# The expert layer of a convolution-attention block: seven block products with sums on VectorE and GpSimd in place of eight, and the next image's tokens turned between the two layers

## Chip, cores and metric

One core of a Trainium2 chip runs the whole program. The metric is the device time in microseconds, the median of several runs. Engine names are short below: PE is TensorE, DVE is VectorE, ACT is ScalarE, Pool is GpSimd, SP is SyncE, which issues nearly all of the DMAs here.

## What is computed

Eight images of 32x32 positions (1024 tokens) with 256 channels pass a convolution with attention, an attention layer, and then a layer of experts with a layer norm. The change is in the experts only. For these the reference has

```python
h = gelu(einsum('nd,edf->enf', xf, W1) + b1[:, None, :])          # D = 256, F = 512, E = 8
y = einsum('enf,efd->end', h, W2) + b2[:, None, :]
out = einsum('ne,end->nd', w_dense, y)                             # two experts of eight have a weight
out = layer_norm(out + x, gamma, beta)
```

The routing is worked out from the mean of an image, so all 1024 tokens of an image use the same two experts. The kernel computes just these two. All numbers are float32.

## The kernel before, in words

The first 1,923 us of the kernel, the convolution and both attentions, are scheduled by hand and are not touched. They leave the tokens of each image in DRAM (`Td`) and the mean and scale of each token's norm in `mv2`.

The stage of the experts (from line 1243) is written as a plain loop over the images b (from line 1417), in which the framework orders the instructions: each engine gets its instructions one after another from a list, by the place that they have in the program. One that is not ready, because its data or a buffer of its pool is missing, is passed by, and a later one goes ahead. The order is fixed when the kernel is built; on the chip every engine works through its own queue in order. A pool's `bufs` says how many buffers a tile name has. A buffer is given to the next tile when the last reader of the tile before it is done.

For image b the loop does this:

- `load_image(b + 1)` (line 1273) has SP load the next image's tokens `T2` (1 MB), and `load_experts(b + 1)` (line 1376) the two experts' `w1` and `w2` (512 KB each); Pool scales `w2` by the routing weight (line 1390). All have two buffers.
- `turn` (line 1278) makes the normed tokens `n2` on DVE (line 1282, eight instructions) and turns them for the matmuls: 16 transposes on PE into four tiles of pool `ps_t` (two buffers), copied out by DVE (line 1293) and ACT (line 1295) into `n2T`, 128 channels x 2 halves of channels (`kc`) x 1024 tokens. For image 0 it is called ahead of the loop, for the others at the head of their own iteration (line 1422).
- `mix` (line 1424) is a small matmul with the experts' second bias. ACT copies it to `mixed`; Pool adds it to `n2` (line 1427) and adds `beta` to `T2` (line 1428).
- Then, for each half q of the tokens (512 of them), the first layer: for each expert k and each of four blocks f of 128 hidden units, two matmuls of 128x128 by 128x512 into `phd` (line 1435, pool `ps_h`, three buffers) and one Gelu with bias on ACT into `hT` (line 1442). After it the second layer of the same half: four groups of eight matmuls into `py` (line 1452, pool `ps_y`, three buffers), whose results DVE adds to `n2` (line 1459, called r below), with the statistics, a square root on ACT (line 1464), and two DVE instructions per group (lines 1468 and 1469, the latter writing `yo`). SP stores `yo` (line 1472).

One float32 matmul appears as two PE records in the profile.

Of the kernel before, what the change touches and what calls it, by code (L numbers as in the profile page):

```python
# [10 lines left out]
FP = mybir.dt.float32  # L11
FR = mybir.dt.float32r
I32 = mybir.dt.int32
AF = mybir.ActivationFunctionType
ALU = mybir.AluOpType
AX = mybir.AxisListType
PSUM = bass.MemoryType.PSUM

P = 128
B, HH, WW, C = 8, 32, 32, 256  # L20
S = HH * WW
NT = S // P
KC = C // P
# [6 lines left out]
NF = F // P  # L30
TOPK = 2
# [7 lines left out]
def kernel(  # L39
# [26 lines left out]
    nc = tc.nc  # L66
# [45 lines left out]
    with ExitStack() as ph:  # L112
        wp = ph.enter_context(tc.tile_pool(name="wp", bufs=1))
        work = ph.enter_context(tc.tile_pool(name="work", bufs=1))
# [39 lines left out]
        def st_tile(name):  # L154
            return ps_st.tile([P, 512], FP, tag="st", name=name)
# [22 lines left out]
        for i, (n, table) in enumerate((("h", key_rel_h), ("w", key_rel_w))):  # L178
# [8 lines left out]
            out=rawc.rearrange("p (m o) -> p m o", o=CO), in_=conv_w.rearrange("a b (k p) o -> p (a b k) o", p=P)  # L187
# [164 lines left out]
        class Fill:  # L352
# [47 lines left out]
            def add(self, work, cost):  # L400
                self.dense.append(work)
                self.owed += cost
# [651 lines left out]
        class Attention:  # L1054
# [27 lines left out]
            def turn(self, last=False):  # L1082
                blk, i, pr = self.scored.pop(0)
                for c in range(2):
                    tp = st_tile("tp").rearrange("p (j t) -> p j t", j=4)
                    for j in range(4):
                        jc = c * 4 + j
                        te.transpose(tp[:, j, :], pr[:, jc * P : (jc + 1) * P], ident)
                    dst = blk.pt[:, c * 4 : c * 4 + 4, i * P : (i + 1) * P]
                    if c == 0 and not last:  # L1090
                        nc.vector.tensor_copy(dst, tp)
                    else:
                        nc.scalar.copy(dst, tp)
                if self.turned:
                    self.turned.pop(0).finish()
                if i == NIB - 1:
                    self.turned.append(blk)
# [146 lines left out]
    fw = ctx.enter_context(tc.tile_pool(name="fw", bufs=2))  # L1244
    work = ctx.enter_context(tc.tile_pool(name="fwork", bufs=2))
    ps_t = ctx.enter_context(tc.tile_pool(name="ps_t", bufs=2, space=PSUM))
    ps_h = ctx.enter_context(tc.tile_pool(name="ps_h", bufs=3, space=PSUM))
    ps_y = ctx.enter_context(tc.tile_pool(name="ps_y", bufs=3, space=PSUM))

    wr = small.tile([P, KC, E], FP, tag="wr", name="wr")  # L1250
    nc.sync.dma_start(out=wr, in_=w_r.rearrange("(k p) e -> p k e", p=P))
# [17 lines left out]
    def sm(shape, name):  # L1269
        return small.tile(shape, FP, tag=name, name=name)  # L1270


    def load_image(b):
        t = work.tile([P, NT, C], FP, tag="T2", name="T2")
        nc.sync.dma_start(out=t, in_=Td[b])
        return t

    def turn(b, Tb):
        n2 = work.tile([P, NT, C], FP, tag="n2", name="n2")
        n2T = work.tile([P, KC, S], FP, tag="n2T", name="n2T")  # L1280
        for t in range(NT):
            nc.vector.tensor_scalar(
                n2[:, t, :], Tb[:, t, :], mv2[:, b, t, 0:1], mv2[:, b, t, 1:2], ALU.subtract, ALU.mult
            )
        for kc in range(KC):
            for q in range(2):
                tp = ps_t.tile([P, 4, P], FP, tag="t", name="tp2")
                for j in range(4):
                    nc.tensor.transpose(tp[:, j, :], n2[:, q * 4 + j, kc * P : (kc + 1) * P], ident)
                dst = n2T[:, kc, q * 512 : (q + 1) * 512]  # L1290
                src = tp.rearrange("p j t -> p (j t)")
                if q == 0:
                    nc.vector.tensor_copy(dst, src)
                else:
                    nc.scalar.copy(dst, src)
        return n2, n2T

    tn = load_image(0)
    plog = ps_t.tile([P, 512], FP, tag="t", name="plog")
# [76 lines left out]
    def load_experts(b):  # L1376
        ws = []
        for k in range(TOPK):
            n = k * B + b
            e = nc.sync.value_load(idx_i[0:1, n : n + 1], min_val=0, max_val=E - 1)  # L1380
            w1t = fw.tile([P, KC, F], FP, tag=f"w1_{k}", name=f"w1_{k}")
            nc.sync.dma_start(
                out=w1t, in_=w1[bass.ds(e, 1), :, :].rearrange("o (k p) f -> p (o k) f", p=P)
            )
            w2t = fw.tile([P, NF, C], FP, tag=f"w2_{k}", name=f"w2_{k}")
            nc.sync.dma_start(
                out=w2t, in_=w2[bass.ds(e, 1), :, :].rearrange("o (f p) d -> p (o f) d", p=P)
            )

            nc.gpsimd.tensor_scalar(w2t, w2t, wbc[:, n : n + 1], None, ALU.mult)  # L1390
            ws.append((w1t, w2t))
        return ws

    nxt = load_experts(0)
    turned = turn(0, tn)
    gelu = sm([B, TOPK], "gelu")
    nc.scalar.activation(gelu, wt, AF.Gelu)
# [16 lines left out]
    b1c = sm([P, NF, TOPK * B], "b1c")  # L1414
    nc.vector.tensor_copy(b1c, pb)

    for b in range(B):
        ws, Tb = nxt, tn
        if b + 1 < B:
            tn = load_image(b + 1)  # L1420
            nxt = load_experts(b + 1)
        n2, n2T = turned if b == 0 else turn(b, Tb)
        mix = ps_t.tile([P, 512], FP, tag="t", name="mix")
        nc.tensor.matmul(mix[:, 0:C], lhsT=dbc[:, b, :], rhs=b2sb, start=True, stop=True)
        mixed = work.tile([P, 1, C], FP, tag="mixed", name="mixed")
        nc.scalar.copy(mixed[:, 0, :], mix[:, 0:C])
        nc.gpsimd.tensor_tensor(n2, n2, mixed.to_broadcast([P, NT, C]), ALU.add)
        nc.gpsimd.tensor_tensor(Tb, Tb, bet.to_broadcast([P, NT, C]), ALU.add)
        for q in range(2):
            hT = work.tile([P, TOPK * NF, 512], FP, tag="hT", name="hT")  # L1430
            for k in range(TOPK):
                for f in range(NF):
                    phd = ps_h.tile([P, 512], FP, tag="h", name="phd")
                    for kc in range(KC):
                        nc.tensor.matmul(  # L1435
                            phd,
                            lhsT=ws[k][0][:, kc, f * P : (f + 1) * P],
                            rhs=n2T[:, kc, q * 512 : (q + 1) * 512],
                            start=kc == 0,
                            stop=kc == KC - 1,  # L1440
                        )
                    nc.scalar.activation(  # L1442
                        hT[:, k * NF + f, :], phd, AF.Gelu, bias=b1c[:, f, k * B + b : k * B + b + 1]
                    )
            r = work.tile([P, 4, C], FP, tag="r", name="r")
            st = work.tile([P, 4, 6], FP, tag="fst", name="fst")
            mv = work.tile([P, 4, 2], FP, tag="fmv", name="fmv")
            for j in range(4):
                py = ps_y.tile([P, C], FP, tag="y", name="py")
                for k in range(TOPK):  # L1450
                    for f in range(NF):
                        nc.tensor.matmul(  # L1452
                            py,
                            lhsT=hT[:, k * NF + f, j * P : (j + 1) * P],
                            rhs=ws[k][1][:, f, :],
                            start=k + f == 0,
                            stop=k == TOPK - 1 and f == NF - 1,
                        )
                nc.vector.tensor_tensor(r[:, j, :], py, n2[:, q * 4 + j, :], ALU.add)  # L1459
                nc.vector.bn_stats(st[:, j, :], r[:, j, :])  # L1460
            for i in range(4):
                nc.vector.bn_aggr(mv[:, i, :], st[:, i : i + 1, :])
            nc.vector.tensor_scalar(mv[:, :, 1], mv[:, :, 1], 1e-5, None, ALU.add)
            nc.scalar.activation(mv[:, :, 1], mv[:, :, 1], AF.Sqrt)
            nc.vector.reciprocal(mv[:, :, 1], mv[:, :, 1])
            y = work.tile([P, 4, C], FP, tag="yo", name="yo")
            for j in range(4):
                nc.vector.scalar_tensor_tensor(r[:, j, :], r[:, j, :], mv[:, j, 0:1], gam, ALU.subtract, ALU.mult)
                nc.vector.scalar_tensor_tensor(
                    y[:, j, :], r[:, j, :], mv[:, j, 1:2], Tb[:, q * 4 + j, :], ALU.mult, ALU.add  # L1470
                )
            nc.sync.dma_start(
                out=ot[b, q * 512 : (q + 1) * 512, :].rearrange("(p k) c -> p k c", k=4), in_=y
            )
# [50 lines left out]
```

## Time and profile before

| | us |
|---|---|
| median of three runs (2415.1, 2431.19, 2431.35) | 2431.19 |
| the profiled execution: its time | 2426.65 |
| its span, first to last instruction | 2424.9 |
| PE busy in the span | 2203.9 |
| DVE busy | 1384.1 |
| ACT busy | 1041.5 |
| Pool busy | 516.6 |
| experts' stage, first matmul of `phd` to the end | 1950.5 to 2424.9 |

The profile has one line per group of instructions: line of the source, engine, operation, output and input by name, shapes and count, then the busy time in us with the mean ns of one, and the idle time of the engine ahead of them with what ended most of it. The windows view gives for a stretch of the span the busy time of PE, of PE's weight loads (PEld), DVE, ACT and Pool, each with its number of instructions, then the granted clock of PE as a share of full speed, and the DMA. The chain view follows the work that ended last back through what released it. The timeline lists start, duration, engine, line and operation.

### The profile page before, as it was taken

How to read it: one execution, taken by the hardware profiler on the slowest of the kernel's cores; microseconds unless marked ns; L12 is line 12 of the kernel's file. 1: busy time of each engine (PE TensorE's matmuls, PEld its weight loads, DVE VectorE, ACT ScalarE, POOL GpSimd, SP SyncE). 2: the span in 40 equal slices, each digit the busy share in tenths (PEclk: the TensorE clock that was granted, in tenths of full speed). 3: DMA queues.
4: the chain of work that ended last, by engine and by line, in shares of the span. 5: the costliest groups of instructions: out<-in, count | busy, mean ns of one | idle time of the engine just before them, and what ended most of it. 6: DMA issues, size and time to landing. Idle time of an engine off the chain costs nothing.

```text
span 2424.9 us, 28815 instructions
## 1 busy us (share of the span) xinstructions
PE 2203.9 (91%) x10515; PEld 1419.0 (59%) x10515; DVE 1384.1 (57%) x3147; ACT 1041.5 (43%) x1990; POOL 516.6 (21%) x446
## 2 busy tenths in 40 slices
PE   5589999899999999999899999999998789999998
PEld 4455556556555665566556556665664456666665
DVE  4667746575685666575657575657571633333333
ACT  2145544444454445444544454445454322222332
POOL 2213211320223022202120311131111042222220
PEclk7699999999999989998999899989998889999999
DMA  4634312701461245124312521361110121222210
GB/s 122 125 88 122 80 40 71 186 11 45 101 152 24 65 108 120 36 70 121 80 36 70 149 52 45 73 166 24 45 45 1 57 87 70 70 70 71 83 46 27
DMA packets 91935, 184.94 MB, mean 76 GB/s; under 512 B 9313, under 2 KB 37866, under 8 KB 90258
## 3 DMA queue, kind: packets, MB, share of 16 engines
q1 hardware_dynamic: 89426, 178.47, 29.2%
q10 hardware_dynamic: 2368, 4.63, 0.8%
q8 instruction: 84, 1.38, 0.2%
q14 instruction: 57, 0.47, 0.1%
HBM read 112.15 MB, written 62.52 MB: 72 GB/s over the span
## 4 chain that ended last, share of the span: by engine, by line
PE 64%; DVE 17%; DMA 7%; ACT 6%; SPq 3%; issue 2%; ACTq 1%; POOL 1%; DVEq 0%; POOLq 0%
PE po L133 11%; PE phd L1435 9%; PE py L1452 9%; PE lg L133 8%; PE st L133 8%; DVE mx L782 7%; PE pc L133 5%; PE pq L133 3%; PE prel L133 2%; DMA F<-mb 2%; ACT PT L826 2%; PE tp L137 2%; PE pa L133 1%; PE pv L133 1%; SPq L586 1%
## 5 line engine op out<-in xcount | busy, mean ns | idle before, releaser
L782 DVE TENSOR_REDUCE mx<-lg 128x1 f32<-128x512 f32 x1024 | 657.8, 686 | 255.7 <-PE lg L133 250.3
L826 ACT ACTIVATE PT<-st 128x512 f32<-128x512 f32 x1024 | 596.9, 598 | 445.2 <-PE st L133 396.3
L133 PE MATMUL st<-F,KM 128*128 128x512 f32 x1024 | 519.2, 512 | 36.1 <-ACT PT L826 23.0
L133 PE MATMUL lg<-KM,F 128*128 128x512 f32 x1024 | 393.6, 422 | 43.1 <-DMA F<-fy 34.6
L133 PEld LDWEIGHTS st<-F,KM 128*128 128x128 f32 x1024 | 198.9, 195 | 243.6 <-ACT PT L826 180.0
L133 PE MATMUL po<-PT,vk 128*32 128x512 f32 x2048 | 282.2, 620 | 0.0
L133 PE MATMUL pc<-convw,V 128*128 128x192 f32 x1152 | 269.7, 337 | 13.4 <-ACT mm L720 12.7
L133 PEld LDWEIGHTS lg<-KM,F 128*128 128x128 f32 x1024 | 200.5, 196 | 92.5 <-issue 39.2
L133 PEld LDWEIGHTS pc<-convw,V 128*128 128x128 f32 x1152 | 211.3, 195 | 60.6 <-issue 19.9
L1435 PE MATMUL phd<-n2T,w 128*128 128x512 f32 x512 | 226.9, 598 | 0.0
L1452 PE MATMUL py<-w,hT 128*128 128x256 f32 x1024 | 223.6, 379 | 0.0
L1452 PEld LDWEIGHTS py<-w,hT 128*128 128x128 f32 x1024 | 194.6, 190 | 33.3 <-issue 7.4
L1459 DVE TENSOR_TENSOR r<-py,n 128x256 f32<-128x256 f32 x64 | 27.2, 425 | 257.5 <-PE py L1452 257.5
L1435 PEld LDWEIGHTS phd<-n2T,w 128*128 128x128 f32 x512 | 96.3, 191 | 113.2 <-issue 109.3
L1065 DVE TENSOR_REDUCE nm<-lg 128x1 f32<-128x512 f32 x128 | 85.4, 686 | 113.2 <-PE lg L133 113.2
L1069 ACT ACTIVATE pr<-lg,nm 128x512 f32<-128x512 f32 x128 | 86.9, 683 | 126.5 <-DVE nm L1066 126.0
L1442 ACT ACTIVATE hT<-phd,b1c 128x512 f32<-128x512 f32 x128 | 86.4, 687 | 101.3 <-PE phd L1435 96.6
L133 PE MATMUL lg<-nqk 128*128 128x512 f32 x256 | 120.7, 594 | 0.0
L133 PE MATMUL po<-pt,v 128*128 128x256 f32 x512 | 115.8, 379 | 0.0
L730 POOL TENSOR_TENSOR ms<-mm 128x192 f32<-128x192 f32 x32 | 19.3, 603 | 446.7 <-ACT mm L720 446.5
L133 PEld LDWEIGHTS po<-pt,v 128*128 128x128 f32 x512 | 95.1, 190 | 11.6
L1390 POOL TENSOR_SCALAR w<-w,wbc 128x1024 f32<-128x1024 f32 x16 | 46.7, 2921 | 252.5 <-DMA w<-in_L_ffn_W_dram 167.8
(259 smaller groups left out, 2501.1 us busy)
## 6 DMA issues: line engine op xcount, KB each, us to landing
F<-fd SPq DMA_DIRECT2D x64, 768.0 KB
F<-fy SPq DMA_DIRECT2D x128, 128.0 KB
w<-in_L_ffn_W_dram SPq DMA_DIRECT2D x32, 512.0 KB
fy<-scr SPq DMA_DIRECT2D x48, 256.0 KB
T<-in_x_dram SPq DMA_DIRECT2D x16, 512.0 KB
fd<-kqh SPq DMA_DIRECT2D x32, 256.0 KB
Td<-T SPq DMA_DIRECT2D x16, 512.0 KB
T<-Td SPq DMA_DIRECT2D x8, 1024.0 KB
```

The source lines that it names most:

```text
L133: nc.tensor.matmul(out, **kw)
L137: nc.tensor.transpose(out, in_, ident)
L586: nc.sync.dma_start(out=qs.bitcast(FP)[32 * i : 32 * i + 32, g], in_=kqb_[DK + 32 * g : DK + 32 * g + 32, i // 2, :],)
L782: nc.vector.tensor_reduce(self.mx[:, a, i, hl : hl + 1], lg, AX.X, ALU.max, negate=True)
L826: nc.scalar.activation(self.pts[j][:, hl, :], st, AF.Exp)
L1065: nc.vector.tensor_reduce(nm[:, h : h + 1], lg[h], AX.X, ALU.max, negate=True)
L1069: nc.scalar.activation(pr[:, h * 512 : (h + 1) * 512], lg[h], AF.Exp, bias=nm[:, 2:3], scale=scale, accum_out=rs[:, h, i : i + 1],)
L1390: nc.gpsimd.tensor_scalar(w2t, w2t, wbc[:, n : n + 1], None, ALU.mult)
L1435: nc.tensor.matmul(phd, lhsT=ws[k][0][:, kc, f * P : (f + 1) * P], rhs=n2T[:, kc, q * 512 : (q + 1) * 512], start=kc == 0, stop=kc == KC - 1,)
L1442: nc.scalar.activation(hT[:, k * NF + f, :], phd, AF.Gelu, bias=b1c[:, f, k * B + b : k * B + b + 1])
L1452: nc.tensor.matmul(py, lhsT=hT[:, k * NF + f, j * P : (j + 1) * P], rhs=ws[k][1][:, f, :], start=k + f == 0, stop=k == TOPK - 1 and f == N ...
L1459: nc.vector.tensor_tensor(r[:, j, :], py, n2[:, q * 4 + j, :], ALU.add)
```

## The change

The first layer is done on whole images. The weights of one expert for two neighbouring blocks f and the tokens of one image form two 2x2 arrangements of blocks (a by hidden block and channel half, b by channel half and token half). Their product, four blocks of 128x512, took eight matmuls. It is now put together from seven matmuls (`p1` to `p7`), each on blocks or on sums of blocks, and the results are added up by DVE in the tiles s, u, v, w. Gelu reads these from SBUF. The sums of the weights (`sw`, four instructions of 128x256 per expert) are made by Pool in `load_experts`, those of the tokens (`sums`, four of 128x512 per image, one buffer) by DVE at the end of `turn`. `hT` holds the whole image, in one buffer. `turn` for image b+1 stands between the first and the second layer of image b. `ps_h` has four buffers instead of three, `ps_y` two instead of three.

```diff
-    ps_h = ctx.enter_context(tc.tile_pool(name="ps_h", bufs=3, space=PSUM))
-    ps_y = ctx.enter_context(tc.tile_pool(name="ps_y", bufs=3, space=PSUM))
+    ps_h = ctx.enter_context(tc.tile_pool(name="ps_h", bufs=4, space=PSUM))
+    ps_y = ctx.enter_context(tc.tile_pool(name="ps_y", bufs=2, space=PSUM))
...
-        return n2, n2T
+        sums = work.tile([P, 4, 512], FP, tag="sums", name="sums", bufs=1)
+        b11, b12, b21, b22 = (n2T[:, kc, q * 512 : (q + 1) * 512] for kc in range(KC) for q in range(2))
+        nc.vector.tensor_tensor(sums[:, 0], b12, b11, ALU.subtract)
+        nc.vector.tensor_tensor(sums[:, 1], b22, sums[:, 0], ALU.subtract)
+        nc.vector.tensor_tensor(sums[:, 2], b22, b12, ALU.subtract)
+        nc.vector.tensor_tensor(sums[:, 3], b21, sums[:, 1], ALU.subtract)
+        return n2, n2T, sums
...
-            ws.append((w1t, w2t))
+            sw = fw.tile([P, 4, NF // 2, P], FP, tag=f"sw_{k}", name=f"sw_{k}")
...
+            nc.gpsimd.tensor_tensor(sw[:, 0], a21, a22, ALU.add)
+            nc.gpsimd.tensor_tensor(sw[:, 1], sw[:, 0], a11, ALU.subtract)
+            nc.gpsimd.tensor_tensor(sw[:, 2], a11, a21, ALU.subtract)
+            nc.gpsimd.tensor_tensor(sw[:, 3], a12, sw[:, 1], ALU.subtract)
+            ws.append((w1t, w2t, sw))
...
+    def hidden(hT, w, n2T, sums, k, f, b):
...
+        def gelu(e, q, src):
+            n = k * NF + f + e
+            nc.scalar.activation(
+                hT[:, n, q * 512 : (q + 1) * 512], src, AF.Gelu, bias=b1c[:, f + e, k * B + b : k * B + b + 1]
+            )
+        def product(a, x):
+            out = ps_h.tile([P, 512], FP, tag="h", name="phd")
+            nc.tensor.matmul(out, lhsT=a, rhs=x, start=True, stop=True)
+            return out
+        def add(out, x, y):
+            nc.vector.tensor_tensor(out, x, y, ALU.add)
+        s, u, w, v = (work.tile([P, 512], FP, tag=f"c{i}", name=f"c{i}") for i in range(4))
+        p1 = product(a11, b11)
+        nc.scalar.copy(s, p1)
+        p6 = product(s2, t2)
+        add(u, p6, s)
+        p7 = product(s3, t3)
+        add(w, p7, u)
+        p5 = product(s1, t1)
+        add(v, p5, w)
+        gelu(1, 1, v)
+        add(u, p5, u)
+        p2 = product(a12, b21)
+        add(s, p2, s)
+        gelu(0, 0, s)
+        p4 = product(a22, t4)
+        add(w, p4, w)
+        gelu(1, 0, w)
+        p3 = product(s4, b22)
+        add(u, p3, u)
+        gelu(0, 1, u)
...
-        n2, n2T = turned if b == 0 else turn(b, Tb)
+        n2, n2T, sums = turned
...
+        hT = work.tile([P, TOPK * NF, S], FP, tag="hT", name="hT", bufs=1)
+        for k in range(TOPK):
+            for f in range(0, NF, 2):
+                hidden(hT, ws[k], n2T, sums, k, f, b)
+        if b + 1 < B:
+            turned = turn(b + 1, tn)
         for q in range(2):
-            hT = work.tile([P, TOPK * NF, 512], FP, tag="hT", name="hT")
-            for k in range(TOPK):
-                for f in range(NF):
...
-                        nc.tensor.matmul(
-                            phd,
...
```

More of the change, by code (lines that the diff above doesn't have):

```diff
@@ L1390, in load_experts @@
             nc.gpsimd.tensor_scalar(w2t, w2t, wbc[:, n : n + 1], None, ALU.mult)
-            ws.append((w1t, w2t))
+            sw = fw.tile([P, 4, NF // 2, P], FP, tag=f"sw_{k}", name=f"sw_{k}")
+            (a11, a21), (a12, a22) = (
+                [w1t[:, kc].rearrange("p (f e u) -> p e f u", e=2, u=P)[:, e] for e in range(2)] for kc in range(KC)
+            )
[4 more added lines that the diff above has]
+            ws.append((w1t, w2t, sw))
         return ws
@@ L1415 @@
     nc.vector.tensor_copy(b1c, pb)
+    def hidden(hT, w, n2T, sums, k, f, b):
+        w1t, _, sw = w
+        a11, a12, a21, a22 = (w1t[:, kc, (f + e) * P : (f + e + 1) * P] for e in range(2) for kc in range(KC))
+        b11, b12, b21, b22 = (n2T[:, kc, q * 512 : (q + 1) * 512] for kc in range(KC) for q in range(2))
+        s1, s2, s3, s4 = (sw[:, i, f // 2] for i in range(4))
+        t1, t2, t3, t4 = (sums[:, i] for i in range(4))
+        def gelu(e, q, src):
+            n = k * NF + f + e
+            nc.scalar.activation(
+                hT[:, n, q * 512 : (q + 1) * 512], src, AF.Gelu, bias=b1c[:, f + e, k * B + b : k * B + b + 1]
+            )
+        def product(a, x):
[24 more added lines that the diff above has]
+        gelu(0, 1, u)
     for b in range(B):
@@ L1428 @@
         nc.gpsimd.tensor_tensor(Tb, Tb, bet.to_broadcast([P, NT, C]), ALU.add)
-        for q in range(2):
-            hT = work.tile([P, TOPK * NF, 512], FP, tag="hT", name="hT")
-            for k in range(TOPK):
-                for f in range(NF):
-                    phd = ps_h.tile([P, 512], FP, tag="h", name="phd")
-                    for kc in range(KC):
-                        nc.tensor.matmul(
-                            phd,
[L1437 to L1444, printed above, removed]
+        hT = work.tile([P, TOPK * NF, S], FP, tag="hT", name="hT", bufs=1)
[4 more added lines that the diff above has]
+            turned = turn(b + 1, tn)
+        for q in range(2):
             r = work.tile([P, 4, C], FP, tag="r", name="r")
@@ L1453 @@
                             py,
-                            lhsT=hT[:, k * NF + f, j * P : (j + 1) * P],
+                            lhsT=hT[:, k * NF + f, q * 512 + j * P : q * 512 + (j + 1) * P],
                             rhs=ws[k][1][:, f, :],
```

## The prediction

> **What bounds the kernel now.** I read the page first, then the windows of one image, the chain, the rows of the instructions that the change uses, and the timeline where Pool and DVE meet. PE is the busiest engine over the span:
>
> ```profile
> PE 2203.9 (91%) x10515; PEld 1419.0 (59%) x10515; DVE 1384.1 (57%) x3147; ACT 1041.5 (43%) x1990; POOL 516.6 (21%) x446
> ```
>
> The change touches only the experts. The windows view of one image there (length, then busy time of PE, PEld, DVE, ACT, Pool, the granted clock, DMA) shows PE idle for 58.20 - 57.85 = 0.35 us, at full clock; DVE, ACT and Pool are each busy for about a third or less:
>
> ```profile
> 2010.00:2068.20 58.20, 57.85 (x212) 38.34 (x211) 20.47 (x54) 17.76 (x25) 14.74 (x4) 1.00 0.20 73
> ```
>
> The chain of the same image (start, length, what): the next image comes 2068.20 - 2009.96 = 58.24 us later. 32 records of the first layer take 13.73, so one takes 0.429 us; 64 of the second take 13.83. Only at the head is DVE on the path, 0.42 + 0.70:
>
> ```profile
> 2009.96 0.02 issue
> 2009.99 0.42 DVE r L1459
> 2010.41 0.01 issue
> 2010.42 0.70 DVE n2T L1293
> 2011.13 0.04 issue
> 2011.17 1.09 PE tp L1289 x8
> ...
> 2026.82 13.81 PE py L1452 x64
> 2040.63 13.73 PE phd L1435 x32
> 2054.37 13.83 PE py L1452 x64
> 2068.20 0.02 issue
> ```
>
> So a matmul taken away here is time taken away, as long as DVE and Pool keep up. These rows price what they get:
>
> ```profile
> L656 DVE TENSOR_TENSOR scr<-prel,scr 128x512 fp32r<-128x512 f32 x24 | 16.4, 683 | 13.8 <-ACT scr L653 13.8
> L537 POOL TENSOR_TENSOR tmp<-base 128x256 f32<-128x256 f32 x32 | 21.5, 693 | 1.3
> L1427 POOL TENSOR_TENSOR n<-n,mixed 128x2048 f32<-128x2048 f32 x8 | 36.1, 4516 | 42.7 <-ACT mixed L1426 42.6
> ```
>
> Last, the timeline (start, length) at two places where a Pool addition and a DVE instruction on SBUF data fall together. One `n` takes 4.64 us where its neighbours take 0.40, and four `yo` take 5.93 us where they otherwise take 1.67. Both end as Pool's addition ends. A DVE instruction of this kind waits for the whole Pool instruction, and DVE's queue waits behind it:
>
> ```profile
> 1939.93 4.59 POOL L1428 TENSOR_TENSOR T<-T,bet 128x2048 f32<-128x2048 f32 x1 [16.46 <-ACT wt L1311]
> 1940.03 4.64 DVE L1282 TENSOR_SCALAR n<-T,mv 128x256 f32<-128x256 f32 x1
> ...
> 2362.61 5.93 DVE L1469 SCALAR_TENSOR_TENSOR yo<-r,fmv,T 128x256 f32<-128x256 f32 x4
> 2363.69 4.57 POOL L1427 TENSOR_TENSOR n<-n,mixed 128x2048 f32<-128x2048 f32 x1 [42.65 <-ACT mixed L1426]
> ```
>
> **The change part by part.** *Matmuls.* 28 for 32 per image, two records each: 8 images x 8 records x 0.429 = **-27.5 us**, all on the chain.
>
> *The turning* moves from the head of an image to behind its predecessor's first layer, where PE has the second layer to go on with. Its 16 transposes stay. What goes is PE's wait: 0.35 per image by the windows, at most 1.12 by the chain's DVE pieces. The windows' value counts PE itself: 7 x 0.35 = **-2.5** (to -7.8).
>
> *The additions.* A block of seven products is 14 x 0.429 = 6.0 us of PE. DVE has seven additions, each with one operand from PSUM like L656: 7 x 0.683 and 0.03 between = 5.0 us. ACT has one copy at 0.58 and four Gelus at 0.69 = 3.3 us. PE hides both: nothing. With four buffers `p1` of the next block needs that of `p5`, whose second addition ends 4.9 us into the block, and `p1` starts at 6.0. So DVE may be late by 1.1 us for free; every further us is PE's.
>
> *DVE's queue at the head of an image.* The first additions stand behind the last `r`, statistics, L1468 and `yo`, which end 3.5 us after the last `py` (2417.59 to 2421.11 at the end of the span). `p6` is done 0.43 (mix) + 4 x 0.429 = 2.15 us after it. DVE is 1.4 late, 0.3 more than is free: 7 x 0.3 = **+2.1** (0 to 9.8, nothing or all of it).
>
> *The next image's `n`* (8 x 0.42 = 3.4 us) now stand among or behind the additions, four blocks of which leave DVE 4.0 us. They wait for the load of `T`, which lands 6.1 us after `yo` at 2014.88; in between DVE had nothing else, now additions queue behind such a wait. I take 0.4 per image, since most fits the gaps: 7 x 0.4 = **+2.8** (0 to 7 x 3.4).
>
> *The sums of tokens* (4 x 0.69 = 2.8 us of DVE) read two SBUF tiles and stand ahead of the second layer's `r`. If Pool's addition to `n` runs there, it starts as the transposes end, 3.1 us behind the first layer: one sum is done, the other three and `r` end at 3.1 + 4.5 + 2.1 + 0.4 = 10.2 us. The third `py`, on two buffers, wants the first `r` at 2.1 + 2 x 3.45 = 9.0: 7 x 1.2 = **+8.4** (0, if Pool is elsewhere, to 7 x 4.5).
>
> *Pool* gets 8 x 0.69 = 5.5 us per image on top of 14.7 of 58: nothing by itself. *SP* issues the same loads; `w1` comes free half an image earlier and `w2`, which the next `w1` queues behind, as before: nothing. The single `hT` is written first 4 us after the last `py` has read it: nothing. The square root's table is needed once per image instead of twice, off the path: nothing.
>
> *The first image* waits for its sums before `p6`: 2.8 us, partly while PE waits for `b1c` anyway (first Gelu at 1955.85). I take **+1**, from -4 (the 4.64 us above is on this path, and the order may change) to +5.
>
> Sum: -27.5 - 2.5 + 2.1 + 2.8 + 8.4 + 1 = -15.7. The profiled execution took 2426.65 (span 2424.9 and 1.75 around it), 0.2% under the median 2431.19 and between the runs' 2415.1 and 2431.35: **2411 us**.
>
> [...]
>
> [...] Between 1926 and 1950, where PE is busy for 5.60 of 24 us, the granted clock is 0.52. [...]
>
> **The rivals.** *All of the gain.* Pool's long additions meet no DVE instruction that matters. Then the 8.4 goes, and 2.8 becomes 1: -27.5 - 2.5 + 2.1 + 1 + 1 = -25.9, **2401 us**. For it: in six of seven heads before, `yo` met no long addition. Against: there Pool had `w` first.
>
> *The end of an image locked (slower).* `mix` has no reason to come late any more: transposes held its buffers before. It comes right behind the last `py`, and with 0.43 of matmul, 0.2 of signals and 0.37 of copy on ACT, Pool adds to `n` from 1.1 to 5.6 us. DVE's last L1468 (at 1.24) and the `yo` wait and end at 8.0; the first addition ends at 8.75, and `p4`, which needs its buffer, starts there and not at 4.7. With 0.4 at the next block: 4.5 per image. The 2.1 and the 8.4 fall away: -27.5 - 2.5 + 7 x 4.5 + 2.8 + 1 = +5.3, **2432 us**. It decides from 3.7 per image on (27.5 + 2.5 - 2.8 - 1 = 26.2, over 7). If Pool's addition to `T` follows it there too, 7 x 4.5 more: 2463. For it: the last head above, where no `w` was ahead. Against: `w` or an earlier `mix` can come first.
>
> *The additions wait for Pool as well.* Pool's additions in a first layer are 4.5 + 4.5 + 5.5 = 14.5; with about 3 us free, 8 x 11 = 88: **2485**. Against: reductions from PSUM (L782) keep 684 ns beside Pool.
>
> *The change doesn't do it:* 14 records per block take longer than 0.429. Against: every record here already has its own weight load, hidden at 0.19.
>
> **How the numbers follow.** Forecast 0.38, all of the gain 0.24, locked once 0.22, locked twice 0.08, additions waiting 0.06, no effect 0.02. 2397 to 2440 takes in the first three with the start's bounds and leaves out the last three and a little below: 0.2. The forecast's own range is 2404 to 2423. About 1% is what a measurement can tell: faster is below 2402 (against the execution's 2426.65), most of the second case and the edge of the first, 0.25; slower is above 2451, the last three, 0.16; within 1% is 0.59.
>
> **What would show it.** Records of `phd` 448 for 512 at 0.429; the period of an image in the chain, 58.24 before: 54.4 without stalls, 56.3 by the forecast, 59 if locked. PE idle by image, and whether it lies at the head (additions late) or in the second layer (`r` late). The length of `yo`, L1468 and the sums beside Pool's 4.5. The forecast is wrong if these keep their lengths, or if PE waits where Pool is idle.

## The result, and the profile after

| | before | after |
|---|---|---|
| median of 22 runs each, on the same chips, us | 2420.63 | 2442.81 |
| ratio (95% interval) | | 1.0094 (1.007 to 1.0118) |
| span of the profiled execution, us | 2424.9 | 2452.6 |
| from the routing's first matmul (`plog`) to the end, us | 494.1 | 516.8 |
| one image, from the end of one second layer to the next, us | 58.2 | 61.4 |

The change costs 22.2 us. In the profiled executions the experts' stage became 22.7 us longer, though 27.5 us of matmuls are gone from it. The other 5.0 us between the two spans lie ahead of `plog`, where nothing was changed, and are spread between executions. In the kernel after the change the line numbers are: `n2` (called n in the profile) 1282, the sums of tokens 1299 to 1302, Pool's `w` 1397 and `sw` 1402 to 1405, the products 1449, the additions 1453, the copy of `p1` by ACT 1457, `mix` 1483, Pool's addition to n 1486 and to T 1487, r 1509, statistics 1510 and 1512, `fmv` 1513 to 1515, the two instructions per group 1518 and 1519.

The page's line of engines: PE is still the busiest, with 2201.0 us for 2203.9. It has 64 instructions less and is hardly less busy, so many of those that remain must take longer. DVE has 190 us more.

```profile
PE 2201.0 (90%) x10451; PEld 1415.8 (58%) x10451; DVE 1574.1 (64%) x3403; ACT 1035.8 (42%) x2006; POOL 565.6 (23%) x510
```

The windows view of the kernel after (length, busy time of PE, PEld, DVE, ACT, Pool, granted clock, DMA): a whole image, then pieces of the image before it. In the whole image PE is idle for 61.45 - 57.72 = 3.73 us, and its 57.72 are 2.8 more than the 54.9 that the same work takes below. The pieces show where: PE works 1.41 of 5 us, in the last 0.8 of which the clock is already at half (hence 0.92 on average), then at half clock for 6 us more, and from then on without a gap at full clock, 44.00 of 44.00.

```profile
2080.45:2141.90 61.45, 57.72 (x203) 37.62 (x203) 44.66 (x86) 17.23 (x27) 20.74 (x12) 0.94 0.19 68
2023.00:2028.00 5.00, 1.41 (x3) 0.30 (x2) 4.96 (x8) 0.68 (x2) 5.00 (x3) 0.92 0.05 16
2028.00:2030.00 2.00, 1.91 (x3) 0.88 (x4) 1.90 (x5) 0.49 (x1) 1.92 (x4) 0.50 0.87 291
2030.00:2032.00 2.00, 2.00 (x4) 0.97 (x3) 1.31 (x4) 1.99 (x3) 2.00 (x2) 0.50 0.98 311
2032.00:2034.00 2.00, 2.00 (x3) 0.68 (x3) 0.60 (x1) 1.74 (x4) 1.40 (x1) 0.50 0.47 193
2036.40:2080.40 44.00, 44.00 (x180) 32.02 (x178) 30.34 (x66) 11.53 (x18) 7.51 (x5) 1.00 0.08 26
```

So the loss is at the head of the image. The timeline of the kernel after there (start, length, engine, line): first Pool, then DVE.

```profile
2020.14 4.50 POOL L1486 TENSOR_TENSOR n<-n,mixed 128x2048 f32<-128x2048 f32 x1 [32.49 <-ACT mixed L1485]
2024.62 3.08 POOL L1397 TENSOR_SCALAR w<-w,wbc 128x1024 f32<-128x1024 f32 x1
```

```profile
2019.99 0.18 DVE L1512 BATCH_NORM_AGGREGATE fmv<-fst 128x2 f32<-128x6 f32 x1
2020.20 4.46 DVE L1513 TENSOR_SCALAR fmv<-fmv 128x4 f32<-128x4 f32 x1
2024.58 0.49 DVE L1518 SCALAR_TENSOR_TENSOR r<-r,fmv,gam 128x256 f32<-128x256 f32 x1
2025.00 0.17 DVE L1515 RECIPROCAL fmv<-fmv 128x4 f32<-128x4 f32 x1
2025.20 2.24 DVE L1519 SCALAR_TENSOR_TENSOR yo<-r,fmv,T 128x256 f32<-128x256 f32 x4
2027.36 3.86 DVE L1453 TENSOR_TENSOR c<-phd,c 128x512 f32<-128x512 f32 x6
```

An instruction on four elements per partition, 0.17 us elsewhere, takes 4.46 and ends as Pool's addition to n ends. All of DVE's queue stands behind it. ACT is the second victim: its queue holds the square root, which needs `fmv`, ahead of the copy of `p1`. PE then waits first for that copy and then for the first addition, with slow records behind (2.07 and 1.91 for the two records of one matmul, which take 1.02 at full clock):

```profile
2024.70 0.21 ACT L1514 ACTIVATE fmv<-fmv 128x4 f32<-128x4 f32 x1 [4.64 <-DVE fmv L1513]
2024.81 0.57 ACT L1457 COPY c<-phd 128x512 f32<-128x512 f32 x1
```

```profile
2018.96 0.69 PE L1483 MATMUL mix<-b2sb,dbc 8*128 8x256 f32 x2
...
2020.55 2.74 PE L1449 MATMUL phd<-sums,sw 128*128 128x512 f32 x6
2025.43 1.13 PE L1449 MATMUL phd<-n2T,w 128*128 128x512 f32 x2 [2.15 <-ACT c L1457]
2028.09 2.07 PE L1449 MATMUL phd<-sums,w 128*128 128x512 f32 x2 [1.53 <-DVE c L1453]
2029.96 1.91 PE L1449 MATMUL phd<-n2T,sw 128*128 128x512 f32 x2
```

All seven heads look like this (in the last, PE's waits are 2.20 and 0.95). The bill, image by image: the first, from `plog` to the first head, took 83.20 for 79.14 (+4.1); six images 6 x (61.44 - 58.23) = +19.3; the last 64.9 for 65.5 (-0.6). That is +22.7 us.

The start's +4.1 (instead of -3.4 for its eight matmul records) has the same cause at another place. In the timeline of the kernel after, Pool adds `beta` to the second image's tokens while DVE makes the first image's sums, and the first products on sums wait for it:

```profile
1956.63 4.87 POOL L1487 TENSOR_TENSOR T<-T,bet 128x2048 f32<-128x2048 f32 x1 [0.23 <-DVE n L1282]
```

```profile
1958.09 3.96 DVE L1300 TENSOR_TENSOR sums<-n2T,sums 128x512 f32<-128x512 f32 x1 [0.35 <-ACT n2T L1295]
```

```profile
1962.19 3.63 PE L1449 MATMUL phd<-sums,sw 128*128 128x512 f32 x4 [2.95 <-DVE sums L1300]
```

### The profile page after: what moved, and what is told of

Its sections match the earlier page's. It is cut to its first block, busy times and chain, and to the rows that moved or that the text cites. A ratio compares the mean times of both kernels' runs of the same rounds, so it can differ in the third digit from the quotient of the medians.

```text
span 2452.6 us, 29243 instructions
## 1 busy us (share of the span) xinstructions
PE 2201.0 (90%) x10451; PEld 1415.8 (58%) x10451; DVE 1574.1 (64%) x3403; ACT 1035.8 (42%) x2006; POOL 565.6 (23%) x510
## 4 chain that ended last, share of the span: by engine, by line
PE 63%; DVE 19%; DMA 6%; ACT 6%; SPq 3%; issue 2%; ACTq 1%; POOL 0%; DVEq 0%; POOLq 0%
PE po L133 11%; PE py L1502 9%; PE st L133 8%; PE lg L133 8%; PE phd L1449 8%; DVE mx L782 7%; PE pc L133 5%; PE prel L133 3%; PE pq L133 2%; DMA F<-mb 2%; ACT PT L826 2%; PE tp L137 2%; PE pa L133 1%; PE pv L133 1%; DVE fmv L1513 1%
## 5 line engine op out<-in xcount | busy, mean ns | idle before, releaser
L133 PE MATMUL pc<-convw,V 128*128 128x192 f32 x1152 | 269.8, 337 | 15.7 <-ACT mm L720 15.2
L1453 DVE TENSOR_TENSOR c<-phd,c 128x512 f32<-128x512 f32 x224 | 143.6, 684 | 30.0 <-PE phd L1449 21.0
L1443 ACT ACTIVATE hT<-c,b1c 128x512 f32<-128x512 f32 x128 | 86.5, 716 | 72.9 <-DVE c L1453 72.6
L1155 DVE SCALAR_TENSOR_TENSOR T<-pa,rc,T 128x256 f32<-128x256 f32 x64 | 30.5, 476 | 116.6 <-PE pa L133 116.6
L722 POOL TENSOR_TENSOR T<-T,mm 128x384 f32<-128x384 f32 x16 | 16.0, 1001 | 345.8 <-ACT mm L720 345.7
L1449 PE MATMUL phd<-sums,sw 128*128 128x512 f32 x192 | 91.7, 613 | 3.0 <-DVE sums L1300 3.0
```

The costliest lines, as they stand in the source:

```text
L133: nc.tensor.matmul(out, **kw)
L1155: nc.vector.scalar_tensor_tensor(tt, pa[:, i, :], rc[:, i : i + 1], tt, ALU.mult, ALU.add)
L1443: nc.scalar.activation(hT[:, n, q * 512 : (q + 1) * 512], src, AF.Gelu, bias=b1c[:, f + e, k * B + b : k * B + b + 1])
L1449: nc.tensor.matmul(out, lhsT=a, rhs=x, start=True, stop=True)
L1453: nc.vector.tensor_tensor(out, x, y, ALU.add)
```

## The experiments

The theory from here on: DVE stands still while Pool runs a long addition, at the head of each image, and this late DVE is what costs ("lock theory"). Ratios are to the kernel before, from runs on the same chip, with 95% intervals. "Image" is the mean of the six periods from the `mix` of the second image to that of the last, in the one profiled execution of each kernel.

**The turning alone, eight products** (`e1_eight`). `hidden` calls the old pair of matmuls summed in PSUM, without `sums` and `sw`; `turn` stays between the layers.

```diff
-        p1 = product(a11, b11)
...
+                        nc.tensor.matmul(
+                            phd,
...
         if b + 1 < B:
             turned = turn(b + 1, tn)
```

> The turning moved alone: eight products as before, added up in PSUM, Gelu reads PSUM, no sums of tokens or weights. Lock theory (Pool's long addition to n holds DVE's last instructions of an image, and the first layer's additions behind them): the lock stays, DVE's fmv L1513 still takes about 4.5 us at six or seven heads, but no product waits for DVE, only Gelu behind the square root; PE idles 1 us at most per head, the image takes 58 to 59 us and the ratio to the kernel before is 0.998 to 1.005. Rival (the moved turning by itself costs the time): image over 60 us, ratio over 1.007.

Measured: 2417.08 us, ratio 1.0000 (0.9963 to 1.0038), image 58.36. The same lock is there, and PE hardly sees it. Timelines of this kernel, DVE, then PE:

```profile
2111.19 4.53 DVE L1479 TENSOR_SCALAR fmv<-fmv 128x4 f32<-128x4 f32 x1
```

```profile
2109.94 0.69 PE L1449 MATMUL mix<-b2sb,dbc 8*128 8x256 f32 x2
2110.57 7.13 PE L1433 MATMUL phd<-n2T,w 128*128 128x512 f32 x16
2118.01 4.56 PE L1433 MATMUL phd<-n2T,w 128*128 128x512 f32 x10 [0.31 <-ACT hT L1425]
```

With eight products ACT reads PSUM directly and DVE is not between the matmuls, so 4.5 us of a still DVE cost 0.3. The lock comes with the moved turning; its price comes with the seven products.

**Seven products, turning back at the head** (`e2_head`).

```diff
-        n2, n2T, sums = turned
+        n2, n2T, sums = turned if b == 0 else turn(b, Tb)
...
-        if b + 1 < B:
-            turned = turn(b + 1, tn)
```

> Seven products alone: the turning is called at the head of each image as before. Lock theory: the transposes hold back the mix matmul and w stands ahead on Pool, so fmv L1513 keeps its 0.17 us at most heads; instead p6 waits for the sums behind the transposes, 2 to 3 us of PE per image. The image takes 57 to 59 us against 61.4 in the changed kernel, ratio to the kernel before 0.993 to 1.004. Rival (the seven products with their additions are too slow for DVE anywhere): image over 61 us, ratio over 1.008.

Measured: 2441.77, ratio 1.0087 (1.0055 to 1.0119), image 60.8. The expectation missed; the image lies just under what the rival asked for, the ratio above it. `fmv` takes 0.97 here, but the sums of tokens now stand at the head as well, among DVE's tail and beside Pool's `sw`, and the products on sums wait for them. The timeline of PE in this kernel:

```profile
2141.86 1.10 PE L1449 MATMUL phd<-sums,sw 128*128 128x512 f32 x2 [1.18 <-DVE sums L1300]
2145.42 3.78 PE L1449 MATMUL phd<-sums,sw 128*128 128x512 f32 x4 [2.46 <-DVE sums L1301]
```

So the seven products cost about the same with the turning in its old place, by another wait: what they do is put DVE's queue in PE's path at the head.

**The clock kept up** (`e3_warm`). The kernel after, with four matmuls at each head whose result nobody reads.

```diff
         p5 = product(s1, t1)
+        if b > 0 and k + f == 0:
+            spare = ps_t.tile([P, 512], FP, tag="t", name="spare")
+            for _ in range(4):
+                nc.tensor.matmul(spare, lhsT=a11, rhs=b11, start=True, stop=True)
         add(v, p5, w)
```

> Work added: at the head of every image but the first, four more matmuls of 128x512 (3.43 us at full clock) whose result nobody reads stand on PE between p5 and p2, where PE idled 2.15 us. Theory that the products after the stall are slow by the granted clock (0.50 from 2028 to 2034): PE stays busy, the clock stays at 1.0, the image takes 57.5 to 59.5 us against 61.4 although 3.4 us of matmuls were added, ratio to the kernel before 0.997 to 1.004. Rival (those products are slow because they wait for DVE's additions): clock or not, the image stays at 61 us or grows to 64, ratio 1.009 or more.

Measured: 2444.35, ratio 1.0086 (1.0045 to 1.0127), image 61.7: missed. The windows view of one image (61.90 long) shows the clock at 1.00 all through and nothing won. In the timeline of DVE, further on in the head, its queue waits for the load of the next image's T, which SP issues behind the late `yo`:

```profile
2083.44:2145.34 61.90, 58.86 (x212) 37.90 (x211) 44.68 (x86) 16.98 (x27) 20.51 (x13) 1.00 0.20 67
```

```profile
2097.30 0.41 DVE L1282 TENSOR_SCALAR n<-T,mv 128x256 f32<-128x256 f32 x1 [2.58 <-DMA T<-Td]
```

Taking away the slow clock alone wins nothing. Where it is gone, DVE's queue makes PE wait later.

**`mix` two groups earlier** (`e4_mix_between`). `mix`, its copy and Pool's two additions for image b+1 stand in the second layer of image b, two groups ahead of its last one.

```diff
+                if b + 1 < B and q == 1 and j == 1:
+                    add_biases(b + 1, turned[0], tn)
                 nc.vector.tensor_tensor(r[:, j, :], py, n2[:, q * 4 + j, :], ALU.add)
```

> The mix matmul, its copy and Pool's two additions of the next image stand in the program ahead of the third group of the second half of the second layer, so Pool's addition to n runs 2 to 6 us before the last py ends and not behind it. Lock theory: fmv L1513 goes from 4.5 to 0.17 us, PE does not idle over 0.5 us at the head, the clock stays at 1.0, the image takes 54.5 to 56 us, ratio to the kernel before 0.987 to 0.994. Rival (DVE's own 3.5 us behind the last py are too much for the additions even without the lock): image 58 us or more, ratio over 1.0.

Measured: 2407.86, ratio 0.995 (0.9915 to 0.9985), image 55.6: the image as expected, the ratio 0.001 above the range. The lock is as long as ever, but it holds an instruction for which nobody is waiting, and costs 0.3 per image beside a kernel without the addition (55.3, e6 below). DVE's timeline and the windows view of this kernel:

```profile
2107.59 4.79 DVE L1524 SCALAR_TENSOR_TENSOR r<-r,fmv,gam 128x256 f32<-128x256 f32 x1
2112.30 0.41 DVE L1515 TENSOR_TENSOR r<-py,n 128x256 f32<-128x256 f32 x1
```

```profile
2106.41:2162.13 55.72, 54.88 (x203) 36.27 (x203) 45.15 (x86) 16.92 (x27) 21.02 (x12) 1.00 0.22 76
```

That is 5.8 us less per image, for the same instructions in another order, and a kernel faster than the one before the change.

**No addition, and half of it** (`e6_no_n_add`, `e7_half_add`). Line 1486 is taken out, or works on half of n, so these kernels leave out the experts' second bias in whole or in half. In the second the queues of PE, DVE and ACT are those of the kernel after, instruction by instruction.

```diff
-        nc.gpsimd.tensor_tensor(n2, n2, mixed.to_broadcast([P, NT, C]), ALU.add)
+        nc.gpsimd.tensor_tensor(n2[:, 0:4], n2[:, 0:4], mixed.to_broadcast([P, 4, C]), ALU.add)
```

> The kernel after the change without Pool's addition of the experts' second bias to n (left out of the computation; mix and its copy by ACT stay where they are). Lock theory: the four-element DVE instruction at the head is back at 0.2 us, the image takes 54.5 to 56 instead of 61.4, ratio to the kernel before 0.987 to 0.994. Rival (what costs at the head is mix and ACT's copy, or the additions' place behind DVE's tail, and Pool only coincides): image stays above 59, ratio above 1.003.

> The kernel after the change with Pool adding the bias to half of n only (128x1024, about 2.26 us by 4.5 for 2048; the other half is left out of the computation); the queues of PE, DVE and ACT are the same. Lock theory: the four-element DVE instruction takes about 2.2 us, the first addition comes 2.2 us earlier, p4 starts about 6.8 instead of 9.05 us behind the last py, so the image takes 2.2 us less than 61.4 or a bit more than that, about 58 to 59.5; ratio to the kernel before 0.999 to 1.005. Rival (the price is a fixed one, as of a stall followed by a slow clock): image 61 or more, ratio 1.007 or more.

Measured: without it 2404.03, ratio 0.9927 (0.9889 to 0.9966), image 55.3; with half of it 2410.74, ratio 0.9972 (0.9933 to 1.0012), image 57.0. In the half dose `fmv` takes 2.36 and PE waits 1.53 at one place; its clock stays at 1.00 in all six images (timelines of DVE and PE, windows of one image):

```profile
2050.46 2.36 DVE L1513 TENSOR_SCALAR fmv<-fmv 128x4 f32<-128x4 f32 x1
```

```profile
2056.25 1.12 PE L1449 MATMUL phd<-sums,w 128*128 128x512 f32 x2 [1.53 <-DVE c L1453]
```

```profile
2049.22:2106.04 56.82, 55.24 (x203) 36.10 (x202) 42.21 (x86) 17.12 (x27) 18.57 (x12) 1.00 0.21 75
```

The lock theory holds. But the half costs 1.7 per image, less than expected, and the whole 61.4 - 55.3 = 6.1: the second half is dearer than the first.

**Why the second half is dearer** (`e9_warm_T3`, `e10_T3`, `e12_warm_T3_late`, `e13_T3_late`). Two things come only with the full lock, the half clock and the late load of T. T2 gets a third buffer, so that its load need not wait for `yo`; with the four unread matmuls (e9) and without (e10).

```diff
-        t = work.tile([P, NT, C], FP, tag="T2", name="T2")
+        t = work.tile([P, NT, C], FP, tag="T2", name="T2", bufs=3)
```

> The kernel of e3_warm (the kernel after the change with four unread matmuls at each head) with three buffers instead of two for the tokens T2, so that the next image's load need not wait for the late yo. Theory: the full lock costs 6.1 per image (61.4 against 55.3 without the addition) where 3.7 is PE's own idle time, and the rest is either the slow clock or, where that is taken away, the wait of DVE's queue for T; with both away the image takes 55.3 + 3.7 = 59.0, between 58.3 and 60, ratio to the kernel before 0.998 to 1.004. Against: with T early some of the next image's n (0.42 each) now stand ahead of the first additions. Rival (the 2.4 beyond the idle time has another cause): image 61 or more, ratio 1.006 or more.

> The kernel after the change with three buffers instead of two for T2. Theory of e9_warm_T3: the slow clock stays and takes the place of the wait, so the image stays at 61 to 62 and the ratio at 1.006 to 1.012. Rival (DVE's wait for T alone makes the difference): image 58.5 to 59.5, ratio 0.998 to 1.003.

Measured: e9 2464.34, ratio 1.0159 (1.0096 to 1.0222), image 64.2; e10 2448.02, ratio 1.0138 (1.0069 to 1.0207), image 61.6. The first missed and the second met its image but not its ratio. Taken alone neither answers the question, since the earlier T let the next image's n go ahead in DVE's queue: one of them now takes the lock in front of `fmv`, and others stand in front of the additions (DVE's timeline of e10):

```profile
2059.21 0.40 DVE L1282 TENSOR_SCALAR n<-T,mv 128x256 f32<-128x256 f32 x1
...
2059.62 4.58 DVE L1282 TENSOR_SCALAR n<-T,mv 128x256 f32<-128x256 f32 x1
2064.11 0.16 DVE L1513 TENSOR_SCALAR fmv<-fmv 128x4 f32<-128x4 f32 x1
```

The same two with n held in its old place, behind the first block's additions:

```diff
+        with tc.issue_after(first) if first else nullcontext():
             for t in range(NT):
                 nc.vector.tensor_scalar(
...
-            turned = turn(b + 1, tn)
+            turned = turn(b + 1, tn, ends[0])
```

> e9_warm_T3 with the next image's n kept behind the first block's additions in DVE's queue, where they stand in the kernel after the change. So the clock is kept up by unread matmuls, the load of T is early, and the additions have their old place. Theory (beyond PE's idle time of 3.7 the full lock costs the slow clock or DVE's wait for T, whichever comes later): image 58.3 to 60, ratio to the kernel before 0.997 to 1.004. Rival (another cause): 61 or more, ratio 1.006 or more.

> e10_T3 with the next image's n kept behind the first block's additions. T is early, the clock falls. Theory: the slow clock alone keeps the image at 60.5 to 62, ratio 1.005 to 1.012. Rival (the wait for T is the whole of it, the slow clock costs nothing): 58.3 to 59.5, ratio 0.997 to 1.002.

Measured: e12 (warm, T early) 2435.57, ratio 1.0069 (1.0037 to 1.0102), image 60.2; e13 (T early) 2444.42, ratio 1.0109 (1.0051 to 1.0167), image 61.0, rising from 60.2 to 61.4 within the run. e13 came as its theory expected. e12's image lies between its two expectations, its ratio in the rival's. Its DVE timeline shows no wait for T and a queue that works off its delay without a pause, n among the additions:

```profile
2125.33 4.52 DVE L1520 TENSOR_SCALAR fmv<-fmv 128x4 f32<-128x4 f32 x1
...
2130.38 2.24 DVE L1526 SCALAR_TENSOR_TENSOR yo<-r,fmv,T 128x256 f32<-128x256 f32 x4
2132.54 4.66 DVE L1454 TENSOR_TENSOR c<-phd,c 128x512 f32<-128x512 f32 x7
2137.12 2.40 DVE L1283 TENSOR_SCALAR n<-T,mv 128x256 f32<-128x256 f32 x5
2139.44 0.68 DVE L1454 TENSOR_TENSOR c<-phd,c 128x512 f32<-128x512 f32 x1
```

So of the 6.1 us per image about 60.2 - 55.3 = 4.9 are DVE's delay alone. The other 1.2 go with the slow clock: e13, where T is early, grows image by image from 60.15 to 61.39, e10 comes down from 61.82 to 61.45, and the kernel after stays at 61.44, so in the end T early or late makes no difference there. In the trace of the kernel after, the fall of the clock recurs every 61.44 us from the second image's head on, and up to the last image each fall lasts 6.83 us. Why the images of all three kernels end near the same length was not shown. With the clock kept up the wait for T does count: 61.7 - 60.2 = 1.5.

**Another kind of Pool instruction** (`e8_one_input`). The addition to n becomes one with a single tensor input; all queues keep their order.

```diff
-        nc.gpsimd.tensor_tensor(n2, n2, mixed.to_broadcast([P, NT, C]), ALU.add)
+        nc.gpsimd.tensor_scalar(n2, n2, mixed[:, 0, 0:1], None, ALU.add)
```

> The kernel after the change with Pool's addition to n replaced by one that adds a value per partition (one input of 128x2048 instead of two; it adds the first column of the bias instead of the bias, so the output differs). By the 2.84 us of the scaling of w (128x1024, one input) it takes about 5.7 us, longer than the 4.5 it replaces; all four queues keep their order. Theory that only Pool's instructions with two inputs lock DVE: the four-element DVE instruction takes 0.2 to 1 us, image 54.5 to 57, ratio 0.987 to 0.998. Rival (a long Pool instruction of any kind locks DVE until it ends): that instruction takes about 5.7 us, image 62 to 63.5, ratio 1.010 to 1.016.

Measured: 2433.29, ratio 1.004 (0.9995 to 1.0084), image 58.5. Neither theory. Pool's and DVE's timelines of this kernel:

```profile
2078.20 5.47 POOL L1486 TENSOR_SCALAR n<-n,mixed 128x2048 f32<-128x2048 f32 x1 [28.27 <-ACT mixed L1485]
```

```profile
2078.18 0.17 DVE L1513 TENSOR_SCALAR fmv<-fmv 128x4 f32<-128x4 f32 x1
2078.26 3.95 DVE L1518 SCALAR_TENSOR_TENSOR r<-r,fmv,gam 128x256 f32<-128x256 f32 x1
2082.13 0.17 DVE L1515 RECIPROCAL fmv<-fmv 128x4 f32<-128x4 f32 x1
2082.34 1.67 DVE L1519 SCALAR_TENSOR_TENSOR yo<-r,fmv,T 128x256 f32<-128x256 f32 x4
```

`fmv` had begun before Pool did. The next instruction took 3.95 instead of 0.48 and ended 1.5 us before Pool; then four `yo` kept their 1.67 beside Pool's last 1.3 us. So one tensor input holds DVE too, but not to the end. What decides when it lets go stays open. This kernel also prices the slow clock within one run: three of its six images have 3.41 us at half clock and take 58.77, 58.77 and 58.58; the other three, at full clock all through, take 58.26, 58.33 and 58.33.

**The start, and the best version** (`e5_start`, `e11_start_T3`, `e14_start_T3_late`). e5 is e4 with the additions of `beta` for the first two images queued on Pool behind its first addition to n. e11 adds the third buffer of T2 to e5, e14 the later n to e11 (both edits as above).

```diff
+        last.append(nc.gpsimd.tensor_tensor(n2, n2, mixed.to_broadcast([P, NT, C]), ALU.add))
+        with tc.issue_after(last[0].ins) if b < 2 else nullcontext():
+            nc.gpsimd.tensor_tensor(Tb, Tb, bet.to_broadcast([P, NT, C]), ALU.add)
```

> The kernel of e4_mix_between, with Pool's additions of beta to the tokens of images 0 and 1 (128x2048, 4.6 to 4.9 us each) queued on Pool behind its addition to the first image's n. In the kernel after the change they run from 1944.98 and 1956.63 and end together with an n of 4.63 us (neighbours 0.40) and a sum of 3.96 (neighbours 0.67). Lock theory: both go back to 0.4 and 0.7, the first image begins up to 4 us earlier by the n and its p6 no longer waits 2.95 for the sums, so 3 to 8 us less than e4_mix_between (2407.86 there): ratio to the kernel before 0.991 to 0.994. Rival (the start hangs on the routing and the loads of w, not on these two locks): no change beside e4_mix_between, 0.995.

> The kernel of e5_start with three buffers instead of two for T2. There DVE waits 1.9 us for T at each head and PE 0.8 for an addition. If that wait sets PE's stall the image goes from 55.6 to 55.0 or less, and the ratio to the kernel before from 0.9927 to 0.989 to 0.992; if the earlier n only take the place of the additions in DVE's queue, nothing changes (0.991 to 0.995).

> e11_start_T3 with the next image's n kept behind the first block's additions: nothing of DVE's waits for T, and the additions come first. Image 54.9 to 55.4 for 55.8 in e11_start_T3, ratio to the kernel before 0.986 to 0.990. Rival (the remaining idle time of PE comes from yo and the additions themselves): image 55.6 or more, ratio 0.989 to 0.992.

Measured: e5 2403.91, ratio 0.9927 (0.9882 to 0.9972), image 55.6; e11 2395.52, ratio 0.9896 (0.9848 to 0.9943), image 55.7; e14 2409.48, ratio 0.9942 (0.9911 to 0.9972), image 56.2. From `plog` to the end e4 takes 476.6, e5 472.9, e11 466.2, e14 481.3. e5 came as expected; e11's ratio did so by luck, since its image is not shorter; e14 missed. In e5 both locks at the start are gone, and one of the moved additions found a new victim, a sum for the second image, for which PE then waited 4.60 (DVE's timeline, then PE's):

```profile
1976.35 8.53 DVE L1299 TENSOR_TENSOR sums<-n2T 128x512 f32<-128x512 f32 x1 [0.69 <-ACT n2T L1295]
```

```profile
1987.67 16.53 PE L1509 MATMUL py<-w,hT 128*128 128x256 f32 x64 [4.60 <-DVE r L1518]
```

e11 has no such wait; from `plog` to the second image's `mix` it takes 64.9 us where e5 takes 72.1, and this is its whole gain, since its image is not shorter. That DVE waits for T at the head of e5 costs nothing by that, and e14 agrees: with n held back the image is no shorter either. e14 loses the gain at the start again: from `plog` to the second image's `mix` it takes 77.3, with a wait of PE for a DVE addition of 4.56 in it. e11 is the fastest here: its stage is 494.1 - 466.2 = 27.9 us shorter than before. That this is about what the matmuls promised is partly chance. Its images gain 58.2 - 55.7 = 2.5 each of the 3.4 that their matmuls are worth; the rest lies in the first and the last image, and part of that is the lock of 4.64 at the start, which the kernel before has too and where it was left in place.

## Why the prediction was wrong

The forecast was 15.7 us less, 2411 us; the kernel became 22.2 us slower and, at 2442.81, lies above the upper end of 2440.

*What bounds the kernel, and the matmuls:* right. With the lock out of the way an image takes 54.9 to 55.9 (e6) where 54.4 was said for one without stalls, and 44 us in a row of the kernel after have no gap.

*The lock, as a thing:* right. Beside one of Pool's long two-input additions `fmv` (0.17 us elsewhere) took 4.46 to 4.52 at the heads of the kernel after, and an `n` (0.40) took 4.64 at the start of the kernel before: they stood still until it ended, whatever their own length. The additions from PSUM did not: six took 3.86, 0.64 each, beside a Pool addition of 4.56 (at 2048.61 in the kernel after). That excludes the rival in which additions wait as well.

*The place of the lock: here it failed.* The step on the sums of tokens put Pool's addition to n into the second layer, 1.2 us per image, +8.4. In the kernel after the sums take 0.69 each there, and no r is late, so this term is 0; the addition comes right behind the last `py`, as the rival "the end of an image locked" had it. The forecast gave that 0.22, because `w` had stood first in six of seven heads before. But `w` stood first because `mix` came late, and the same text says that nothing makes `mix` late any more. Once the wait that ordered them is gone, the old order is no evidence: n was first at all seven heads. In e2, where the turning holds `mix` back again, `w` is first again at six of seven heads.

*The price of that rival:* the mechanism was right and the term too small. It said 4.5 per image, `p4` starting 8.75 us behind the last `py`; it started 9.05 behind it. Measured 6.1. DVE's delay by itself cost 4.9 (e12), near the 4.5; 1.2 more go with the slow clock (61.4 against e12's 60.2), for which the 2432 has no term. It also missed ACT: the copy of `p1` waited in ACT's queue behind the square root and cost PE 2.15 of its 3.7 idle us. That this added nothing to the sum is only argued: `p4` waited for the first addition, which came later than the copy.

*DVE's queue at the head* (+2.1) and *the next image's n* (+2.8): small, as said. Without the addition (e6) PE is idle for 0.0 to 1.0 us in an image, 0.4 on average, where the two terms together had 0.7.

*The start* (+1): measured +7.5 beside its matmuls, above its upper end of +5. The row of 4.64 that the text names was at this place, and a second of its kind came on top. e5 and e11 take both away. The first of the two is in the kernel before as well, so it explains none of the +7.5. Of this, 1.7 come ahead of the first product (21.4 us after `plog` for 19.7) and 2.95 are PE's wait for the second; the rest was not traced to its cause.

*The turning* (-2.5): not gained by itself. In e1 PE still idles 0.31 in an image where it idled 0.35 before, now behind ACT and the lock instead of behind the turning; the image stays at 58.4 and the ratio at 1.0000.

The difference to the forecast goes into two places: per image 61.4 for 56.3, over six images 31 us, and at the start 6.5.

## What to carry to other kernels

Before a cheap operation goes to Pool, or a stage to DVE, look for every pair of Pool addition and DVE instruction on SBUF data that can fall together, and ask who waits behind DVE just there; the same 4.5 us cost 0.3 (e1, e4) or 6.1 (the kernel after) per image here, by what stood behind them. When a change takes away a wait, the order of what stood behind that wait is open again, and must be worked out anew instead of being read from the old trace. If the order is free, put a long Pool addition where DVE works only from PSUM (its additions kept to 0.64 us each beside one of 4.56), or where nobody waits for DVE; here the second alone turned 0.9% slower into 0.5% faster.

## What the runs showed of the hardware

- A DVE instruction on four elements per partition took 4.46 to 4.53 us (the kernel after, e1) because Pool ran a two-input addition of that length, and 2.36 beside one of half the length (e7). Beside short Pool additions (`sw`, 0.72 alone) both took longer: 1.17 to 1.21 each for Pool, 1.21 each for DVE's sums, which take 0.69 alone (1961 to 1966 in the kernel after). Held in this way were DVE instructions with two SBUF inputs (a sum, 3.96 in the kernel after; four `yo`, 5.93 for 1.67 in the kernel before) and with one (`n`, 4.64; `fmv`); the additions with one operand from PSUM were not (0.64 each beside a Pool addition of 4.56), nor was a reciprocal of 8x1 in SBUF that began 0.03 behind Pool's addition (0.14, at 1939.96 in the kernel before). What it is in an instruction that decides this was not shown. A single-input Pool instruction of 5.47 us held DVE for 3.95 of them (e8).
- In the traces of the kernels before and after, every stretch at half clock that lies inside the span lasts 3.41 us or a multiple of it (18 stretches before, 28 after). In the kernel after, TensorE's granted clock fell to 0.50 about 2027.2, after an idle time of 2.15 us, 1.13 of work and 0.6 of a second idle time, and came back 6.83 us later. A single idle time of 2.54 (e8) was followed by a fall at three heads, for 3.41 us each, and by none at two others, so the length of the gap alone does not decide. After one of 1.53 alone the clock stayed at 1.00 (e7). In the 3.41 us ahead of a fall PE was busy for 33% in the kernel after and for 25 to 35% in e8's heads; what makes the clock fall was not shown. A fall of 6.83 us went with 1.2 per image (61.4 against e12's 60.2), one of 3.41 us with 0.3 to 0.5 (e8).
